# Convolution, two attentions and a mixture of experts: the expert stage begins with the image that is still on chip

## The chip, the cores and the metric

The kernel runs on one core of one Trainium2 chip. The metric is the device time in microseconds (us). The time before is 2335.57 us, the median of three runs (2335.0 to 2337.08). The engines of the core are named as the profile names them: PE multiplies matrices, and PEld is its loading of weights; DVE is the vector engine, ACT the scalar engine with its function tables, POOL is GpSimd, and SP only issues transfers.

## What is computed

Eight images of 32 x 32 pixels and 256 channels, all in 32-bit floats, pass two layers. The reference, cut to what matters here:

```python
# layer 0: group norm, 3x3 convolution (192 channels) beside 8-head attention (64 channels), residual
x = x + _L0_conv_ref(_gn(x), ...)
# layer 1: one-head attention on 1024 tokens of 256, then a mixture of experts
t = _to_tokens(x)
t = t + _L1_attn_ref(_ln_t(t), ...)
t = t + _L1_ffn_ref(_ln_t(t), ...)

def _L1_ffn_ref(x, Wr, br, W1, b1, W2, b2, gamma, beta):
    logits = jnp.mean(x, axis=1) @ Wr + br          # one row per image
    routing_weights = softmax(logits)
    expected_loads = routing_weights.sum(axis=0) * (N / B)
    scale = jnp.where(expected_loads > capacity, capacity / expected_loads, 1.0)
    routing_weights = softmax(routing_weights * scale)
    top_w, top_i = jax.lax.top_k(rw_tok, 2)         # the same two experts for all tokens of an image
    top_w = softmax(top_w)
    h = gelu(x @ W1[e] + b1[e])                     # 256 -> 512
    y = h @ W2[e] + b2[e]                           # 512 -> 256
    out = sum over the two experts of top_w * y
    return _layer_norm(out + x, gamma, beta)
```

The router takes the mean over the tokens of each normalised image, and the load of an expert is a sum over all eight images: no expert is known until the last image has left the attention.

## The kernel before

**Stages.** A loop over the images b = 0 to 7 does the convolution layer with its attention (`conv_layer_attention`) and the one-head attention (`attention_layer`), with the work of the next image filled in. An image is a tile `T[b]` of 128 x 8 x 256: eight tiles t of 128 tokens. At the end of `attention_layer` the last output tiles come from `gather` (L932) and `project` (L944, L948 to L950), which also leaves the mean and variance of every token in `mv2`. Then `root_of_tiles` (L96 to L102, two of its steps on ACT) makes one over the deviation of all eight tiles, and `mr` is mean times that. The sum over tokens of image times deviation is collected in `acc`: on POOL for images 0 to 6 (L983, L985), on DVE for image 7 (L987, L989). The image is stored to DRAM in `Td[b]` by POOL's queue (L990). `token_mean` (L995 to L1003) finishes the sum over partitions with two products on PE against ones, and `mr` with one more, and writes a column of `meanT`.

**Router.** On 8 x 8 numbers, mostly DVE: logits (L1132), a softmax (L1140 to L1144), the loads (L1151 to L1159), a second softmax, and twice the search for the largest: maximum, candidates, smallest index, one-hot row `oh`, picked weight. The indices go through PE (L1196) into the integers `idx_i`; `wbc` holds the experts' weights spread over the partitions, `dbc` the dense weights of the bias, `b1c` the chosen first biases.

**Expert stage.** For b = 0 to 7: the image comes back from `Td[b]` (L1228, loaded one image ahead on SP), SP reads the two experts of an image from `idx_i` and loads 512 KB each of first and second weights (L1237, L1241), one image ahead, in two buffers. `n2` is the normalised image (L1265, eight DVE operations), `n2T` its transpose: 16 transposes on PE into the PSUM pool `ps_t` with two buffers (L1272), copied out by DVE (L1276) and ACT (L1278). `pbr` (L1281) is the experts' second bias; POOL adds it to `n2` and beta to the image (L1286, L1287) and scales the next second weights by `wbc` (L1251). For each half q of the tokens, PE makes the hidden layer `phd` for two experts and four column groups (L1296; ACT applies Gelu, L1303), then four output tiles `py` (L1313, PSUM pool `ps_y` with three buffers); DVE adds `n2` (L1320), takes statistics (L1321), and when all four tiles of the half are there `layer_stats` makes one over the deviation (L86 to L90, the root on ACT), two operations a tile finish it (L1325, L1326), and one 512 KB transfer writes it out (L1329).

**Order.** In the loop over images PE and POOL run in the order in which the program is written (L1045); in the expert stage only POOL does (L1253), and the order of the other engines comes from a scheduler at compile time. On SP, ACT and DVE it is the scheduler's in both stages. [...]

Of the kernel before, what the change touches and what calls it, by code (L numbers as in the profile page):

```python
# [10 lines left out]
FP = mybir.dt.float32  # L11
# [25 lines left out]
def kernel(  # L37
# [38 lines left out]
    Td = [dram.tile([P, NT, C], FP, tag=f"Td{b}", name=f"Td{b}") for b in range(B)]  # L76
# [27 lines left out]
    with ExitStack() as ph:  # L104
# [24 lines left out]
        def load_image(b):  # L129
            t = work.tile([P, NT, C], FP, tag="T", name="T", bufs=2)  # L130
            eng = nc.gpsimd if b else nc.sync
            eng.dma_start(
                out=t.rearrange("p (r j) c -> p r j c", j=4), in_=xt[b].rearrange("(r p j) c -> p r j c", p=P, j=4)
            )
            return t
# [678 lines left out]
        def root_of_tiles(var):  # L814
            one_over_root(var, var, lambda n: work.tile([P, NT, 1], FP, tag=f"{n}t", name=n))

        def attention_layer(b, fill, conv, maxima):
# [133 lines left out]

            for i in range(NT):
# [17 lines left out]
            conv.run(2)  # L970
            project(NT // NIB - 1, os)


            m = mv2[:, b]
            root_of_tiles(m[:, :, 1:2])
            mr = work.tile([P, NT], FP, tag="mr", name="mr")
            nc.vector.tensor_tensor(mr, m[:, :, 0], m[:, :, 1], ALU.mult)
            acc = work.tile([P, C], FP, tag="n", name="acc", bufs=2)
            if b + 1 < B:
                part = work.tile([P, C], FP, tag="n", name="part", bufs=2)  # L980
                for t in range(NT):
                    to = part if t else acc
                    nc.gpsimd.tensor_scalar(to, T[b][:, t, :], m[:, t, 1:2], None, ALU.mult)  # L983
                    if t:
                        nc.gpsimd.tensor_tensor(acc, acc, part, ALU.add)  # L985
            else:
                nc.vector.tensor_scalar(acc, T[b][:, 0, :], m[:, 0, 1:2], None, ALU.mult)  # L987
                for t in range(1, NT):
                    nc.vector.scalar_tensor_tensor(acc, T[b][:, t, :], m[:, t, 1:2], acc, ALU.mult, ALU.add)  # L989
            nc.gpsimd.dma_start(out=Td[b], in_=T[b])  # L990
            return acc, mr

        def token_mean(b, acc, mr):

            pmt = st_tile("pmt")  # L995
            for kc in range(KC):
                nc.tensor.matmul(
                    pmt[:, kc : kc + 1], lhsT=acc[:, kc * P : (kc + 1) * P], rhs=ones[:, 0:1], start=True, stop=True
                )
# [3 lines left out]
            nc.vector.tensor_scalar(meanT[:, :, b], pmt[:, 0:KC], mrs, 1.0 / S, ALU.subtract, ALU.mult)  # L1003
# [41 lines left out]
        with tc.manual_schedule(engines={mybir.EngineType.PE, mybir.EngineType.Pool}):  # L1045
            conv = Conv(0)
            means = []
            for b in range(B):
# [49 lines left out]
                del T[b]  # L1098
# [25 lines left out]
    nc.vector.tensor_copy(iota, iota_i)  # L1124
# [21 lines left out]

    rw = sm([B, E], "rw")
# [20 lines left out]
    for k in range(TOPK):  # L1168
# [3 lines left out]
        nc.vector.tensor_scalar(cand, z, m, -float(E), ALU.is_equal, ALU.mult)  # L1172
        nc.vector.tensor_tensor(cand, cand, iota, ALU.add)
        nc.vector.tensor_reduce(idx[:, k : k + 1], cand, AX.X, ALU.min)
        nc.vector.tensor_scalar(idx[:, k : k + 1], idx[:, k : k + 1], float(E), float(E - 1), ALU.add, ALU.min)
        oh = sm([B, E], f"oh{k}")
        nc.vector.tensor_scalar(oh, iota, idx[:, k : k + 1], None, ALU.is_equal)
        hot.append(oh)
        pick = sm([B, E], f"pick{k}")
        nc.vector.tensor_tensor(pick, oh, rw2, ALU.mult)  # L1180
        nc.vector.tensor_reduce(top[:, k : k + 1], pick, AX.X, ALU.add)
        if k + 1 < TOPK:
            off = sm([B, E], f"off{k}")
            nc.vector.tensor_scalar(off, oh, 4.0, None, ALU.mult)
            z2 = sm([B, E], f"z{k}")
            nc.vector.tensor_tensor(z2, z, off, ALU.subtract)
            z = z2
    wt = sm([B, TOPK], "wt")
    softmax(wt, top, "sm3")


    prow = ps_t.tile([P, 512], FP, tag="t", name="prow")
    pw = ps_t.tile([P, 512], FP, tag="t", name="pw")
    diag = sm([B, TOPK, B], "diag")
    for k in range(TOPK):
# [3 lines left out]
        nc.vector.tensor_scalar(diag[:, k, :], ident[0:B, 0:B], wt[:, k : k + 1], None, ALU.mult)  # L1199
    nc.tensor.matmul(  # L1200
        pw[:, 0 : TOPK * B], lhsT=ones[0:B], rhs=diag.rearrange("p k b -> p (k b)"), start=True, stop=True
    )
    idx_i = small.tile([1, TOPK * B], I32, tag="idx_i", name="idx_i")
    nc.vector.tensor_copy(idx_i, prow[0:1, 0 : TOPK * B])
    wbc = sm([P, TOPK * B], "wbc")
    nc.vector.tensor_copy(wbc, pw[:, 0 : TOPK * B])
    dense = sm([B, E], "dense")
    nc.vector.tensor_scalar(dense, hot[0], wt[:, 0:1], None, ALU.mult)
    nc.vector.scalar_tensor_tensor(dense, hot[1], wt[:, 1:2], dense, ALU.mult, ALU.add)
    ptr = ps_t.tile([P, 512], FP, tag="t", name="ptr")  # L1210
    for i, m in enumerate((hot[0], hot[1], dense)):
        nc.tensor.transpose(ptr[0:E, i * B : (i + 1) * B], m, ident[0:B, 0:B])
    hotT = sm([E, (TOPK + 1) * B], "hotT")
    nc.vector.tensor_copy(hotT, ptr[0:E, 0 : (TOPK + 1) * B])
    dbc = sm([E, B, P], "dbc")
    nc.vector.tensor_copy(dbc, hotT[:, TOPK * B :].unsqueeze(2).to_broadcast([E, B, P]))

    pb = ps_t.tile([P, NF, TOPK * B], FP, tag="t", name="pb")
    for f in range(NF):
        nc.tensor.matmul(  # L1220
            pb[:, f, :], lhsT=b1sb[:, f * P : (f + 1) * P], rhs=hotT[:, 0 : TOPK * B], start=True, stop=True
        )
    b1c = sm([P, NF, TOPK * B], "b1c")
    nc.vector.tensor_copy(b1c, pb)

    def load_image(b):
        t = work.tile([P, NT, C], FP, tag="T2", name="T2")
        nc.sync.dma_start(out=t, in_=Td[b])  # L1228
        return t

    def load_experts(b):
        ws = []
        for k in range(TOPK):
            n = k * B + b
            e = nc.sync.value_load(idx_i[0:1, n : n + 1], min_val=0, max_val=E - 1)
            w1t = fw.tile([P, KC, F], FP, tag=f"w1_{k}", name=f"w1_{k}")
            nc.sync.dma_start(  # L1237
                out=w1t, in_=w1[bass.ds(e, 1), :, :].rearrange("o (k p) f -> p (o k) f", p=P)
            )
            w2t = fw.tile([P, NF, C], FP, tag=f"w2_{k}", name=f"w2_{k}")  # L1240
# [3 lines left out]
            ws.append((w1t, w2t))  # L1244
# [8 lines left out]
    ctx.enter_context(tc.manual_schedule(engines={mybir.EngineType.Pool}))  # L1253
    nxt = load_experts(0)
    scale_experts(0, nxt)
    tn = load_image(0)
    for b in range(B):
        ws, Tb = nxt, tn
        if b + 1 < B:
            tn = load_image(b + 1)  # L1260
            nxt = load_experts(b + 1)
        n2 = work.tile([P, NT, C], FP, tag="n2", name="n2")
        n2T = work.tile([P, KC, S], FP, tag="n2T", name="n2T")
        for t in range(NT):
            nc.vector.tensor_scalar(  # L1265
                n2[:, t, :], Tb[:, t, :], mv2[:, b, t, 0:1], mv2[:, b, t, 1:2], ALU.subtract, ALU.mult
            )
        for kc in range(KC):
            for q in range(2):
                tp = ps_t.tile([P, 4, P], FP, tag="t", name="tp2")  # L1270
                for j in range(4):
                    nc.tensor.transpose(tp[:, j, :], n2[:, q * 4 + j, kc * P : (kc + 1) * P], ident)  # L1272
                dst = n2T[:, kc, q * 512 : (q + 1) * 512]
                src = tp.rearrange("p j t -> p (j t)")
                if q == 0:
                    nc.vector.tensor_copy(dst, src)  # L1276
                else:
                    nc.scalar.copy(dst, src)  # L1278
# [104 lines left out]
```

## Time and profile before

The profile is one execution that took 2339.52 us, of which 2337.5 us lie between the first and the last instruction (the span). All times below are us from the start of the span.

| stretch | time | PE busy | DVE busy | ACT busy | POOL busy | PE clock | transfers, GB/s |
|---|---|---|---|---|---|---|---|
| 1750 to 1842: end of the last image's attention | 92.0 | 80.37 | 32.69 | 40.28 | 10.56 | 0.91 | 1 |
| 1842 to 1870.2: token mean, router, first transposes | 28.2 | 9.98 | 19.84 | 2.27 | 4.68 | 0.56 | 227 |
| 1870.2 to 1929.1: experts, image 0 | 58.9 | 58.90 | 14.76 | 16.86 | 16.73 | 0.98 | 53 |
| 1929.1 to 2274.8: images 1 to 6 | 345.7 | 345.70 | 159.25 | 106.47 | 93.91 | 1.00 | 70 |
| 2274.8 to 2337.5: image 7 and the end | 62.7 | 55.31 | 25.18 | 17.96 | 9.77 | 0.97 | 26 |

A row gives how long each engine was busy in the stretch. "PE clock" is the share of full speed that was granted to PE. Busy time of PE counts matmuls whose ends are modelled, so a full row doesn't mean that PE works at its peak; it does mean that no gap is seen between its instructions. A line of a timeline gives start, duration, engine and line, the operation, the tile that it writes and those that it reads, their shapes, and in brackets the idle time before it and what ended that.

### The profile page before, as it was taken

The numbers are of one execution on the slowest core, as the hardware profiler recorded it, in microseconds if no ns is written. First come the engines' busy times: TensorE is split into PE (matmuls) and PEld (weight loads), VectorE is DVE, ScalarE is ACT, GpSimd is POOL, SyncE is SP. The second block draws the span as 40 slices with busy tenths as digits, with TensorE's granted clock in tenths as the row PEclk, the third lists the DMA queues.
The fourth block names the chain that finished last, engine by engine and source line by source line (L and its number), as shares of the span: only waits on it lengthen the run. The fifth ranks groups of instructions, "written<-read, shape, count | busy, mean of one in ns | idle before, by whom it ended". The sixth has DMA issues, their size and how long they took to land. (4 is left out here: it accounts for less than half of the span.)

```text
span 2337.5 us, 41910 instructions
## 1 busy us (share of the span) xinstructions
PE 2259.4 (97%) x17273; PEld 1284.4 (55%) x17273; DVE 1481.7 (63%) x2717; ACT 955.1 (41%) x1645; POOL 505.3 (22%) x478
## 2 busy tenths in 40 slices
PE   5999999999999999999999999999998699999998
PEld 5535753664367437733763475357533566666665
DVE  7777587658756775777477748765872624444443
ACT  2255336434643563256325532553364223333332
POOL 3301240213031203300340034012301022222220
PEclk7999999999999999999999999999998799999999
DMA  3520352125122502250333025202420312222200
GB/s 105 103 50 10 58 104 39 41 48 102 22 56 42 109 5 60 56 93 3 60 89 61 7 56 105 45 27 47 82 38 1 108 50 78 78 74 78 72 37 27
DMA packets 71471, 135.85 MB, mean 58 GB/s; under 512 B 12001, under 2 KB 24169, under 8 KB 69233
## 3 DMA queue, kind: packets, MB, share of 16 engines
q1 hardware_dynamic: 65488, 115.47, 23.5%
q0 software_dynamic: 3056, 15.73, 2.0%
q8 instruction: 137, 2.24, 0.4%
q10 hardware_dynamic: 2736, 1.97, 0.3%
q14 instruction: 54, 0.43, 0.1%
HBM read 53.43 MB, written 25.17 MB: 34 GB/s over the span
## 5 line engine op out<-in xcount | busy, mean ns | idle before, releaser
L626 DVE TENSOR_REDUCE my<-lg 128x32 f32<-128x1024 f32 x512 | 617.4, 1222 | 166.3 <-PE st L658 124.9
L666 ACT ACTIVATE PT<-st 128x512 f32<-128x512 f32 (+1 forms) x944 | 542.2, 632 | 313.6 <-PE st L658 309.9
L658 PE MATMUL st<-F,km 32*128 32x512 f32 x2048 | 536.9, 640 | 8.2 <-DMA F<-mb 8.2
L618 PE MATMUL lg<-km,F 24*128 24x512 f32 x2048 | 504.9, 637 | 1.7 <-DMA F<-rh 1.7
L675 PE MATMUL po<-PT,vall 128*32 128x256 f32 (+1 forms) x3200 | 312.5, 452 | 2.4 <-ACT PT L666 2.4
L675 PEld LDWEIGHTS po<-PT,vall 128*32 128x32 f32 x3200 | 66.0, 108 | 312.8 <-issue 279.5
L618 PEld LDWEIGHTS lg<-km,F 24*128 24x128 f32 x2048 | 144.1, 183 | 163.7 <-issue 122.7
L560 PE MATMUL pc<-convw,gdif 128*128 128x192 f32 x1152 | 229.4, 342 | 0.7 <-ACT convw L309 0.7
L1296 PE MATMUL phd<-n2T,w 128*128 128x512 f32 x512 | 223.7, 595 | 0.0
L1313 PE MATMUL py<-w,hT 128*128 128x256 f32 x1024 | 223.6, 379 | 0.0
L658 PEld LDWEIGHTS st<-F,km 32*128 32x128 f32 x2048 | 175.6, 183 | 78.2 <-issue 40.5
L560 PEld LDWEIGHTS pc<-convw,gdif 128*128 128x128 f32 x1152 | 186.9, 192 | 56.4 <-issue 32.0
L1313 PEld LDWEIGHTS py<-w,hT 128*128 128x128 f32 x1024 | 194.6, 190 | 33.3 <-issue 7.7
L340 POOL TENSOR_TENSOR T<-T,l0b 128x2048 f32<-128x2048 f32 x8 | 36.3, 4534 | 617.6 <-PE tpx L333 617.6
L1320 DVE TENSOR_TENSOR r<-py,n 128x256 f32<-128x256 f32 x64 | 27.2, 425 | 213.0 <-PE py L1313 213.0
L1296 PEld LDWEIGHTS phd<-n2T,w 128*128 128x128 f32 x512 | 97.2, 191 | 116.1 <-issue 108.9
L846 POOL TENSOR_TENSOR T<-T,n 128x256 f32<-128x256 f32 x64 | 47.4, 749 | 392.4 <-DVE n L832 392.4
L1303 ACT ACTIVATE hT<-phd,b1c 128x512 f32<-128x512 f32 x128 | 86.3, 686 | 98.3 <-PE phd L1296 98.1
L569 ACT COPY m<-pc 128x384 f32<-128x384 f32 x48 | 23.0, 480 | 242.6 <-PE pc L560 198.1
L901 PE MATMUL lg<-qkv 128*128 128x512 f32 x256 | 121.1, 595 | 0.0
L910 DVE TENSOR_REDUCE nm<-lg 128x1 f32<-128x1024 f32 x64 | 78.1, 1221 | 67.5 <-PE lg L901 67.5
L932 PE MATMUL po<-pt,qkv 128*128 128x256 f32 x512 | 116.5, 380 | 0.0
(250 smaller groups left out, 2584.7 us busy)
## 6 DMA issues: line engine op xcount, KB each, us to landing
F<-rh SPq DMA_DIRECT2D x256, 128.0 KB
F<-kq SPq DMA_DIRECT2D x256, 64.0 KB
F<-rwd SPq DMA_DIRECT2D x256, 64.0 KB
w<-in_L_ffn_W_dram SPq DMA_DIRECT2D x32, 512.0 KB
rwd<-rw SPq DMA_DIRECT2D x16, 512.0 KB
Td<-T POOLq DMA_DIRECT2D x8, 1024.0 KB, 4.2
T<-Td SPq DMA_DIRECT2D x8, 1024.0 KB
out_dram<-yo SPq DMA_DIRECT2D x16, 512.0 KB
```

What stands on the lines that cost most here:

```text
L560: nc.tensor.matmul(pc[:, v, :], lhsT=gflat[:, 2 * pair + v, kc, at : at + P], rhs=convw[:, 2 * pair + v, dy, kc * CO : (kc + 1) * CO], sta ...
L618: nc.tensor.matmul(lg[:, a, :], lhsT=self.F[r : r + 24, a, 0, i * P : (i + 1) * P], rhs=KM[self.g][r : r + 24, a].rearrange("p e k -> p (e ...
L626: nc.vector.tensor_reduce(my[:, :, hl], lg.rearrange("p a (y x) -> p y a x", y=WW), AX.XY, ALU.max)
L658: nc.tensor.matmul(st[:, i, :] if len(heads) > 1 else st, lhsT=KM[self.g][r : r + 32, a, e, :], rhs=self.F[r : r + 32, a, e, :], start=Tru ...
L666: nc.scalar.activation(self.pts[j][:, hs, :], st, AF.Exp)
L675: nc.tensor.matmul(self.po[32 * hl : 32 * hl + 32, cols], lhsT=vall[:, j, h * (DH + 1) : h * (DH + 1) + 32], rhs=self.pts[j][:, hl, cols], ...
L901: nc.tensor.matmul(lg[:, h, :], lhsT=qk[0][:, i * P : (i + 1) * P], rhs=qk[1][:, h * 512 : (h + 1) * 512], start=True, stop=True,)
L910: nc.vector.tensor_reduce(nm, lg, AX.X, ALU.max, negate=True)
L932: nc.tensor.matmul(po[:, 0:IB], lhsT=v1[:, jc, :], rhs=pt[:, jc, :], start=jc == 0, stop=jc == NT - 1)
L1296: nc.tensor.matmul(phd, lhsT=ws[k][0][:, kc, f * P : (f + 1) * P], rhs=n2T[:, kc, q * 512 : (q + 1) * 512], start=kc == 0, stop=kc == KC - 1,)
L1303: nc.scalar.activation(hT[:, k * NF + f, :], phd, AF.Gelu, bias=b1c[:, f, k * B + b : k * B + b + 1])
L1313: nc.tensor.matmul(py, lhsT=hT[:, k * NF + f, j * P : (j + 1) * P], rhs=ws[k][1][:, f, :], start=k == 0 and f == 0, stop=k == TOPK - 1 and ...
```

## The change

The seven parts below all lie between the end of the last image's attention and the end of the kernel, apart from `token_mean`, which all images use.

1. The images' tiles get a pool of their own (`tokens`, two buffers), which the expert stage uses too. The last image is neither stored nor loaded again; the expert stage takes the images in the order 7, 0, 1, ..., 6. Image 0 is loaded before the stage begins, into the buffer that image 6 has left.
2. The last image's sum over tokens is made by PE: for each tile and each half of the channels one product of the tile with the column of one over the deviation, summed in PSUM. The first six tiles come before the last `project`, the last two after it. The deviations are made in the same two parts.
3. In `token_mean` two DVE operations write `meanT`, one for each half of the channels, where there was one.
4. From the router on, DVE, PE and POOL run in the order in which the program is written.
5. In the router the candidates are one operation instead of two (`iota` holds the index minus 8), so are the numbers for the second search, and the picked weights, the third softmax and everything that hangs on them stand behind the indices. `weigh_experts` (diag, `pw`, `wbc`, dense weights, `dbc`) stands between the first and the second expert of the first image; so do the transposes of that image's second half.
6. In the expert stage the first weights of both experts are loaded ahead of the second weights. The bias product, the additions on POOL and the scaling stand behind the first expert of the first half (`beside`). The next image is normalised after the first half's hidden layer and transposed between the second and the third output tile of the second half.
7. At the very end the last half is finished in two steps: three output tiles, then the fourth, each with its own transfer.

```diff
@@ attention_layer, end
+            def sum_tiles(part):
+                if not sums_of:
+                    sums_of.extend(lg_tile(f"pm{kc}")[:, 0, :] for kc in range(KC))
+                for t in range(part.start, part.stop):
+                    for kc in range(KC):
+                        nc.tensor.matmul(
+                            sums_of[kc][:, 0:1],
+                            lhsT=T[b][:, t, kc * P : (kc + 1) * P],
+                            rhs=mv2[:, b, t, 1:2],
+                            start=t == 0,
+                            stop=t == NT - 1,
+                        )
...
             conv.run(2)
+            if b + 1 == B:
+                deviation(slice(0, NT - NIB))
+                sum_tiles(slice(0, NT - NIB))
             project(NT // NIB - 1, os)
...
+                nc.gpsimd.dma_start(out=Td[b], in_=T[b])
             else:
-                nc.vector.tensor_scalar(acc, T[b][:, 0, :], m[:, 0, 1:2], None, ALU.mult)
-                for t in range(1, NT):
-                    nc.vector.scalar_tensor_tensor(acc, T[b][:, t, :], m[:, t, 1:2], acc, ALU.mult, ALU.add)
-            nc.gpsimd.dma_start(out=Td[b], in_=T[b])
+                deviation(last_two)
+                sum_tiles(last_two)
+                acc = sums_of
@@ router
+    ctx.enter_context(
+        tc.manual_schedule(engines={mybir.EngineType.DVE, mybir.EngineType.PE, mybir.EngineType.Pool})
+    )
...
-        nc.vector.tensor_scalar(cand, z, m, -float(E), ALU.is_equal, ALU.mult)
-        nc.vector.tensor_tensor(cand, cand, iota, ALU.add)
+        nc.vector.scalar_tensor_tensor(cand, z, m, iota, ALU.is_equal, ALU.mult)
...
+    first = two_tiles()
+    normalised(B - 1, last, range(4), first[0])
+    transposed(*first, 0)
...
+    def weigh_experts():
+        normalised(B - 1, last, range(4, NT), first[0])
+        transposed(*first, 1)
+        pw = ps_y.tile([P, 512], FP, tag="y", name="pw")
+        diag = sm([B, TOPK, B], "diag")
+        for k in range(TOPK):
+            nc.vector.tensor_scalar(diag[:, k, :], ident[0:B, 0:B], wt[:, k : k + 1], None, ALU.mult)
+        nc.tensor.matmul(
+            pw[:, 0 : TOPK * B], lhsT=ones[0:B], rhs=diag.rearrange("p k b -> p (k b)"), start=True, stop=True
+        )
+        nc.vector.tensor_copy(wbc, pw[:, 0 : TOPK * B])
...
@@ expert stage
+    images = [B - 1, *range(B - 1)]
...
+                if q == 0 and k == 0:
+                    if not at:
+                        weigh_experts()
+                    beside()
+            if q == 0 and after is not None:
+                coming = two_tiles()
+                normalised(after, tn, range(NT), coming[0])
...
+            ends = (3, 4) if after is None and q else (4,)
             for j in range(4):
+                if j == 2 and q and after is not None:
+                    for half in range(2):
+                        transposed(*coming, half)
...
+                if j + 1 not in ends:
+                    continue
+                lo = 0 if j + 1 == ends[0] else ends[0]
+                layer_stats(st[:, lo : j + 1], mv[:, lo : j + 1], j + 1 - lo, 1e-5)
...
+                nc.sync.dma_start(out=to[:, lo : j + 1], in_=y[:, lo : j + 1])
```

The new helper `transposed`, for one half q of the tokens:

```python
    def transposed(n2, n2T, q):
        for kc in range(KC):
            tp = ps_t.tile([P, 4, P], FP, tag="t", name="tp2")
            for j in range(4):
                nc.tensor.transpose(tp[:, j, :], n2[:, q * 4 + j, kc * P : (kc + 1) * P], ident)
            dst = n2T[:, kc, q * 512 : (q + 1) * 512]
            src = tp.rearrange("p j t -> p (j t)")
            if kc == 0:
                nc.vector.tensor_copy(dst, src)
            else:
                nc.scalar.copy(dst, src)
```

## The prediction

> **What bounds the kernel now.** I read the engine totals and the 40 slices of the page first: TensorE (PE) is the bound nearly everywhere, and only slices 30 and 31 (58 us each) show it idle and its clock throttled.
>
> ```profile
> PE 2259.4 (97%) x17273; PEld 1284.4 (55%) x17273; DVE 1481.7 (63%) x2717; ACT 955.1 (41%) x1645; POOL 505.3 (22%) x478
> ...
> PE   5999999999999999999999999999998699999998
> ...
> PEclk7999999999999999999999999999998799999999
> ```
>
> Then the timeline of PE there and in the expert stage (start, duration, line, idle time before it and who ended it):
>
> ```profile
> 1841.17 1.13 PE L944 MATMUL pa<-wo,os 128*128 128x256 f32 x4 [0.52 <-ACT os L936]
> 1849.79 1.01 PE L997 MATMUL pmt<-ones,acc 128*128 128x1 f32 x4 [7.48 <-DVE acc L989]
> ...
> 1870.24 15.20 PE L1296 MATMUL phd<-n2T,w 128*128 128x512 f32 x32
> 1885.27 13.98 PE L1313 MATMUL py<-w,hT 128*128 128x256 f32 x64
> ...
> 1926.63 1.04 PE L1272 MATMUL tp<-ident,n 128*128 128x128 f32 x8
> 1927.60 0.69 PE L1281 MATMUL pbr<-b2sb,dbc 8*128 8x256 f32 x2
> 1928.22 1.09 PE L1272 MATMUL tp<-ident,n 128*128 128x128 f32 x8
> 1929.15 13.90 PE L1296 MATMUL phd<-n2T,w 128*128 128x512 f32 x32
> ```
>
> Two things are to be seen. Between the last attention matmuls (1841.2) and the first expert matmul (1870.24) lie 29 us in which PE mostly waits for DVE. From there it never waits: image after image has a period of 57.62 us (1929.15 to 1986.77), of which 2.52 us (1926.63 to 1929.15) are the 16 transposes and the bias matmul `pbr` between two images. What is saved ahead of 1870 is saved at the end; whatever is added to PE's stream after it is added, seven times if it is in the image loop.
>
> **Part by part.** Only the last image's attention tail, the router and the expert stage change.
>
> *Token mean by PE.* Now DVE sums eight tiles (L987 and L989, 1845.74 to 1849.74) and meanT is ready at 1851.70. Changed: PE sums twelve products of the first six tiles before L944, four of the last two after it. A product is two passes; with the clock full, four such passes of L997 cost 0.50 us (the next line's weights start at 322.80, theirs at 322.30), so 0.125 each. Twenty-four passes are 3.0 us, from 1840.5: L944 starts at 1843.5, 2.3 later. Their root fits in DVE's idle time after 1839.0 (row L96 to L102: 1.47 us). Behind L944 DVE's chain keeps its length up to the root (1845.63 now, 1847.93 then), then eight passes (1.0), the last product to meanT (1850.60 to 1851.70: 1.10) and one more 0.22 us meanT operation: 1850.3. **Saves 1.4 us**; 0.6 if the clock has fallen by then (0.22 a pass, as in the L997 row above). The other seven images get one more 0.22 us meanT operation, beside PE-bound work: nothing.
>
> *Router.* From the second softmax's differences (1855.18) to the indices `idx_i` (1859.04) are 3.86 us. Fused candidates, the sums of picked weights moved behind, and no n tiles between save about 1.3; but the fixed order puts the reciprocal and the scaling, which wait for ACT until 1855.54, ahead of the maximum: +0.8. **Saves 0.5.** `idx_i` then ends at 1857.1.
>
> *First expert matmul.* The first weights go out 1.21 us after `idx_i` (1859.04, 1860.25), so at 1858.35. For their landing the nearest rows are the windows of the DMA: 0.5 MB needs till about 2.9 us after its issue, and a wait ends 1.3 us after the data (flow ends at 1944.6, DVE goes on at 1945.96): 1862.5. Transposed input: pb (1.89 us, 1863.61 row) after hotT from 1857.8, eight cold transposes (1.97), the second copy on ACT (0.59): 1862.3. **Matmuls from 1862.5 instead of 1870.24.**
>
> *What follows it.* Here the gain is mostly given back. (a) Clock: the first three passes now come 0.86 us apart instead of 0.43 until 1872.9, a loss of 1.3, after five us of small PE work just ahead. The Trainium skill, "TensorE: Matmul & The Clock Gate", section "The HAM clock gate", says that full speed comes only after a busy window of about 3.4 us of a free-running clock; with little work ahead that is 3.4 to 6.8 us at half speed, a loss of 1.7 to 3.4. By the row 1.3, by the rule some 2.2; I take 2.2, since the change removes the work that the row's window held. (b) Between the first and second expert, `weigh_experts` puts a serial chain into PE's queue: 8 transposes (1.04), with DVE's copy ending at +1.35, diag (0.35), pw, its copy and two dense operations (to +2.85), a transpose, hotT and dbc (0.67; to +4.0), pbr (0.43): 4.5 us in which PE does 1.7. Lower bound 2.5 (if the copies didn't queue), upper 6 (clock falls again). First L1313: 1862.5 + 6.87 + 2.2 + 4.5 + 6.87 = 1882.9, against 1885.27: **−2.3**. POOL scales the second weights (2 × 2.85) from 1874.0 to 1879.7, before they are used; that they are loaded behind both first weights costs nothing for the same reason. The store of the last image, no longer made, held up only the load that is gone too.
>
> *Transposes inside the loop.* They move from between two images to between the second and third output tile of the second half, both halves in a row, with two PSUM buffers. The third group needs the buffer that DVE's copy frees, and in the fixed order that copy stands behind this tile's sum and statistics:
>
> ```profile
> 2295.70 0.42 DVE L1320 TENSOR_TENSOR r<-py,n 128x256 f32<-128x256 f32 x1 [1.76 <-PE py L1313]
> 2296.16 0.43 DVE L1321 BATCH_NORM_STATS2 fst<-r 128x6 f32<-128x256 f32 x1
> ...
> 2273.92 0.85 PEld L1272 LDWEIGHTS tp<-ident,n 128*128 128x128 f32 x8 [0.33 <-DVE n2T L1276]
> ```
>
> PE's slots of that tile end at 2295.49 (2288.59 + 32 × 0.2157). The copy would run from 2296.62 to 2297.31, +1.82; PE goes on 0.26 later (now: copy ends 2273.66, weights 2273.92), and eight transposes take 0.95: 3.03. With pbr elsewhere (0.45): 3.5 instead of 2.52, now filled by pbr and by transposes of the other half. **+0.97 an image, seven times: +6.8**; 5.4 if PE goes on at once.
>
> *Moved loads.* Image 0 is loaded into image 6's buffer, behind the third fold's F<-mb (1720.95) and ahead of the last fold's in SP's queue; the DMA is busy 2% there (1720 to 1752), and the buffer's last use is long past: nothing. If it were not, that fold would stand behind it and PE wait at L658. Later images' loads go out when the previous image's last tiles are done, +7 us in an image, and land by +13 (6.3 us, 1939.63 to 1945.96); L1265 needs them before the first sum at +17.4. The skill ("SBUF — State Buffer", "Who interferes with whom") says that a DVE tensor_scalar in a two-port mode, and DVE operations with two SBUF inputs, stand still for a whole GpSimd operation. The second shows here: L1326 takes up to 2.58 us against 0.48. The first does not: 0.41 us each, and two took 0.73 while POOL scaled (1867.19). By the rule L1265's eight would end near +24, by the row at +16; py has three buffers, its fourth tile starts at +24.1, so either costs PE nothing.
>
> *Last sums.* After the third tile DVE normalises three (six operations near 0.45), so the fourth's sum starts 5.1 us after the third tile instead of 3.66, and the last output is ready 4.6 us after PE ends instead of 3.76 (2329.94, 2333.70): +0.8. The last transfer has 128 KB instead of 512 (1.35 us of data): −1.0. **−0.2.**
>
> *Sum:* −2.3 + 6.8 − 0.2 = +4.3, on a span of 2337.5 (profiled time 2339.5). The median of the runs is 2335.57, 4 below; the same difference gives **2339.9** (+0.18%).
>
> **Rivals.**
> 1. *The transposes don't stall* (the copy gets ahead of the statistics, or a release is quicker): 7 × (2.4 − 2.52) = −0.8, total −3.3: 2332.3. For it: PE has slack for nothing else. Against it: DVE's order is fixed by hand. Faster beyond the bound only if the chain in `weigh_experts` also costs under 3.2 us instead of 4.5.
> 2. *Slower, by the clock*: PE is so little busy in that chain that the clock falls; the second expert's first passes are then at half speed, +2.2, and with weights 1 us late +7.5: 2343. It decides from the point where no window of 3.4 us has enough work; the trace shows the clock falling 3.4 us after the last matmul (1842.3, half by 1845.8), so with gaps under 1 us I hold it the weaker.
> 3. *The early load does harm*: PE waits at L658 in the last fold for 1 MB ahead of it, +5: 2345. Against: 25 us of quiet between the folds.
>
> **Numbers.** Forecast 0.58, rival 1 0.2, rival 2 0.14, rival 3 and the unseen 0.08. A measurement of this kernel tells from no change about 0.2% (4.7 us). The forecast lies just under it, its own range +2 to +7 splits half and half; rival 1 is mostly within, a part faster; 2 and 3 are slower. Slower 0.48, same 0.39, faster 0.13. Range 2332.5 to 2345.5.
>
> **What would show it.** First L1296-like matmul near 1862.5; a PE gap near 4.5 us between the two experts of the first image; in every other image 3 us for the block of transposes with an idle wait on DVE's n2T copy; L944 near 1843.5; the last output about 4.6 us after PE. Wrong if the block takes 2 us, if the first py starts before 1880, or if the stretch before 1839 moves.

## The result, and the profile after

The changed kernel takes 2346.48 us (median of five, 2342.33 to 2347.55) against 2335.57 (median of five too, 2335.00 to 2337.08): a ratio of 1.0043, 95% interval 1.0028 to 1.0058. Measured again (e5 below, 12 runs against 27) the ratio is 1.0029, interval 1.0019 to 1.0039, or 6.8 us. It is slower, as the likeliest sign said, by more than the 4.3 us forecast, and the first median lies outside the range; the second, 2344.48, lies inside.

The page of the profiled execution (2346.51 us, span 2344.7) against the lines shown of before:

```profile
PE 2267.7 (97%) x17301; PEld 1288.0 (55%) x17301; DVE 1473.8 (63%) x2723; ACT 956.0 (41%) x1648; POOL 501.8 (21%) x477
...
PE   5999999999999999999999999999998799999998
...
PEclk7999999999999999999999999999998899999999
```

PE is busy 8.3 us longer with only 28 more instructions: the page sees a slower PE, not more work. Where it is slower, only the timeline tells. PE there, from the last attention work to the second expert of the image that now comes first:

```profile
1848.06 1.87 PE L974 MATMUL pm<-mv,T 128*128 128x1 f32 x8 [3.37 <-DVE mv L107]
...
1862.72 8.55 PE L1377 MATMUL phd<-n2T,w 128*128 128x512 f32 x16 [1.47 <-DVE sm_s L1216]
1871.11 1.04 PE L1187 MATMUL tp<-ident,n 128*128 128x128 f32 x8
1872.75 0.39 PE L1304 MATMUL pw<-diag,ones 8*128 8x16 f32 x2 [0.60 <-DVE diag L1303]
1874.64 0.17 PE L1312 MATMUL ptr<-ident,dense 8*8 8x8 f32 x1 [1.50 <-DVE dense L1310]
1875.77 1.14 PE L1361 MATMUL pbr<-b2sb,dbc 8*128 8x256 f32 x2 [0.96 <-DVE dbc L1314]
```

The first expert starts at 1862.72 instead of 1870.24. Then come three waits for DVE, and the second expert begins only at 1876.83. The granted clock in this stretch (columns: window, its length, busy time and instructions of PE, PEld, DVE, ACT, POOL, then PE's clock, DMA share, GB/s):

```profile
1872.00:1874.00 2.00, 0.54 (x4) 0.29 (x2) 1.48 (x6) 0.59 (x1) 0.54 (x1) 1.00 0.33 107
1874.00:1876.00 2.00, 0.40 (x2) 0.31 (x3) 1.70 (x4) 0.00 (x0) 2.00 (x1) 0.97 0.00 0
1876.00:1878.00 2.00, 2.00 (x4) 0.84 (x4) 2.00 (x3) 0.37 (x1) 2.00 (x2) 0.50 0.00 0
1878.00:1880.00 2.00, 2.00 (x4) 0.86 (x3) 2.00 (x5) 0.00 (x0) 2.00 (x1) 0.50 0.00 0
1880.00:1882.00 2.00, 2.00 (x3) 0.67 (x2) 2.00 (x2) 0.69 (x1) 2.00 (x2) 0.50 0.00 0
```

PE is busy 0.94 us of the first four, and from 1876 the clock is half. The second expert's 16 passes take 9.88 us (1876.83 to 1886.71) instead of 6.97, which the same work takes in e1 below.

To compare profiles whose earlier parts differ, I count from the start of the last attention `po` (L938; L932 before), the last work of PE that no kernel here touches. Times in us; "first py" is the first output tile's first pass.

| profile | that po starts | to 1st expert | 1st expert | between | 2nd expert | to first py | first to last py | last py to end |
|---|---|---|---|---|---|---|---|---|
| before | 1837.04 | 33.20 | 15.03 with 2nd | - | - | 48.23 | 430.86 | 21.37 |
| before, again (e10) | 1832.63 | 33.22 | 14.97 with 2nd | - | - | 48.19 | 430.87 | 21.31 |
| after | 1837.30 | 25.42 | 8.39 | 5.72 | 9.88 | 49.41 | 437.46 | 20.53 |
| after, again (e5) | 1836.76 | 24.94 | 8.92 | 5.29 | 8.66 | 47.81 | 437.46 | 20.57 |

("Last py" is the start of the last 64-pass block.) In the profiled pair the stage is +1.18 up to the first py, +6.60 over the images and -0.84 at the end: +6.94, and with 0.26 ahead of it the 7.2 us between the spans. In the second profile of after it is -0.42, +6.60, -0.80: +5.4. Two profiles of before agree to 0.09 us; those of after differ by 1.6 us, and that is the length of the second fall: 1.22 us in the second expert and 0.43 in `pbr` ahead of it. (The first expert starts 0.48 later in the first profile and takes 0.53 less, because the clock comes back 2.9 us behind its start there, at 1865.6, and 4.0 behind it in e5, at 1865.7.)

The other part of the 10.9 us lies in code that the change doesn't touch. PE's clock also falls elsewhere, in one execution and not in another. Windows of after, then of the first profile of before, then of its second:

```profile
316.00:320.00 4.00, 4.00 (x28) 3.02 (x27) 3.73 (x5) 0.36 (x1) 3.67 (x6) 1.00 0.09 17
320.00:324.00 4.00, 4.00 (x20) 2.14 (x21) 2.85 (x7) 1.80 (x4) 3.31 (x4) 0.85 0.54 131
324.00:328.00 4.00, 4.00 (x17) 2.56 (x12) 1.82 (x3) 1.78 (x4) 0.00 (x0) 0.50 0.95 242
...
328.00:332.00 4.00, 4.00 (x14) 0.72 (x16) 1.78 (x3) 1.09 (x2) 0.00 (x0) 0.50 1.04 161
```

```profile
60.00:64.00 4.00, 2.28 (x7) 0.85 (x6) 0.48 (x1) 1.20 (x2) 3.08 (x4) 0.97 0.60 129
64.00:68.00 4.00, 4.00 (x9) 2.50 (x9) 1.97 (x2) 0.00 (x0) 0.00 (x0) 0.50 0.55 85
```

```profile
60.00:64.00 4.00, 3.50 (x12) 1.48 (x11) 0.73 (x1) 1.54 (x2) 2.66 (x4) 1.00 0.61 132
64.00:68.00 4.00, 4.00 (x23) 2.46 (x22) 1.82 (x3) 0.00 (x0) 0.41 (x1) 1.00 0.55 82
```

The fall in after makes the stretch of L623 to L680 behind it last 33.7 us (320.02 to 353.70) where before takes 29.1. Before's first profile (2339.52 us) lost some 3.2 us against its second (2334.98) around 64, and 1 us more at another fall, from 1753.4 to 1756.8; the last po is 4.4 us apart and everything behind it the same.

So the change itself is worth 5.4 to 6.9 us by the profiles, 6.8 by the ratio of e5. The other 4 us or so of the first comparison are of the size of such falls: the first five times of before lie at 2335 to 2337, while 27 later ones have a median of 2339.41 (2334.34 to 2340.99); of after, four lie at 2346 to 2348 and one at 2342.33. Which of those ten times had which fall is not recorded, except for the one that was profiled, so this part is argued and not shown.

### The profile page after: what moved, and what is told of

It reads as the page before. It is cut to its first block, busy times and chain, and to the rows that moved or that the text cites. A ratio compares the mean times of both kernels' runs of the same rounds, so it can differ in the third digit from the quotient of the medians.

```text
span 2344.7 us, 41981 instructions
## 1 busy us (share of the span) xinstructions
PE 2267.7 (97%) x17301; PEld 1288.0 (55%) x17301; DVE 1473.8 (63%) x2723; ACT 956.0 (41%) x1648; POOL 501.8 (21%) x477
## 5 line engine op out<-in xcount | busy, mean ns | idle before, releaser
L623 PE MATMUL lg<-km,F 24*128 24x512 f32 x2048 | 506.4, 639 | 0.3 <-DMA F<-rh 0.3
L680 PE MATMUL po<-PT,vall 128*32 128x256 f32 (+1 forms) x3200 | 312.6, 452 | 2.9 <-ACT PT L671 2.4
L680 PEld LDWEIGHTS po<-PT,vall 128*32 128x32 f32 x3200 | 66.1, 108 | 314.3 <-issue 280.5
L623 PEld LDWEIGHTS lg<-km,F 24*128 24x128 f32 x2048 | 144.9, 183 | 162.5 <-issue 125.3
L1377 PE MATMUL phd<-n2T,w 128*128 128x512 f32 x512 | 228.9, 603 | 1.5 <-DVE sm_s L1216 1.5
L938 PE MATMUL po<-pt,qkv 128*128 128x256 f32 x512 | 116.5, 380 | 0.0
```

The source lines that it names most:

```text
L623: nc.tensor.matmul(lg[:, a, :], lhsT=self.F[r : r + 24, a, 0, i * P : (i + 1) * P], rhs=KM[self.g][r : r + 24, a].rearrange("p e k -> p (e ...
L680: nc.tensor.matmul(self.po[32 * hl : 32 * hl + 32, cols], lhsT=vall[:, j, h * (DH + 1) : h * (DH + 1) + 32], rhs=self.pts[j][:, hl, cols], ...
L938: nc.tensor.matmul(po[:, 0:IB], lhsT=v1[:, jc, :], rhs=pt[:, jc, :], start=jc == 0, stop=jc == NT - 1)
L1377: nc.tensor.matmul(phd, lhsT=ws[k][0][:, kc, f * P : (f + 1) * P], rhs=n2T[:, kc, q * 512 : (q + 1) * 512], start=kc == 0, stop=kc == KC - 1,)
```

## The experiments

All start from after's code (e10 from before's). The same columns for the changed kernels:

| profile | ratio to before, interval | to 1st expert | 1st expert | between | 2nd expert | to first py | first to last py | last py to end |
|---|---|---|---|---|---|---|---|---|
| e1 busy PE | 1.0022 (1.0016 to 1.0029) | 25.18 | 8.85 | 5.32 | 6.97 | 46.32 | 437.46 | 20.58 |
| e2 chain spread | 1.0001 (0.9992 to 1.0009) | 25.01 | 10.99 with between | - | 6.97 | 42.97 | 437.47 | 20.61 |
| e3 transposes split | 1.0000 (0.9991 to 1.0008) | 25.05 | 8.80 | 5.33 | 8.58 | 47.76 | 431.22 | 20.58 |
| e4 one end | 1.0033 (1.0020 to 1.0045) | 25.01 | 8.90 | 5.28 | 8.66 | 47.85 | 437.47 | 23.29 |
| e5 after again | 1.0029 (1.0019 to 1.0039) | 24.94 | 8.92 | 5.29 | 8.66 | 47.81 | 437.46 | 20.57 |
| e6 e2 and e3 | 0.9965 (0.9952 to 0.9978) | 25.05 | 10.83 with between | - | 6.97 | 42.85 | 431.21 | 20.59 |
| e7 sum by DVE | 1.0031 (1.0021 to 1.0041) | 26.12 | 9.93 | 5.28 | 8.67 | 50.00 | 437.45 | 20.54 |
| e8 dense first | 1.0013 (1.0005 to 1.0022) | 25.00 | 8.70 | 3.78 | 8.67 | 46.15 | 437.46 | 20.56 |
| e9 e6, busy PE | 0.9977 (0.9969 to 0.9984) | 26.50 | 9.00 with between | - | 6.97 | 42.47 | 431.21 | 20.59 |
| e11 e6, busy otherwise | 0.9963 (0.9949 to 0.9977) | 24.02 | 9.51 with between | - | 6.97 | 40.50 | 431.21 | 20.56 |
| e12 e6 again | 0.9985 (0.9978 to 0.9992) | 25.15 | 10.69 with between | - | 6.97 | 42.81 | 431.21 | 20.58 |

Ratios carry the falls elsewhere too; the trace columns are the finer instrument, and the verdicts below rest on them. Each row is one execution: e6 and e12, the same kernel, differ by 0.14 us at most in these columns, and after's two profiles as said above.

**e1: the chain as it is, PE kept busy in its waits.**

```diff
         transposed(*first, 1)
+        busy(1)          # then busy(3) behind pw, busy(2) behind the transpose of dense
...
+def busy(n):
+    spare = ps_h.tile([P, 512], FP, tag="h", name="spare")
+    for _ in range(n):
+        nc.tensor.matmul(spare[:, 0:256], lhsT=ws[0][0][:, 0, 0:P], rhs=n2T[:, 0, 0:256], start=True, stop=True)
```

> The kernel after, with six idle-filling matmuls (128x256, two passes of 0.216 us each, their sums unused) put into PE's three waits inside weigh_experts: one after the transposes, three after pw, two after the transpose of dense. The chain of DVE operations is not touched. Clock theory (PE too little busy there, so that the clock falls at 1875.9 and the second expert's first seven passes come 0.86 apart): the clock stays full, the second expert takes 6.9 us instead of 9.9, the first py starts near 1883.3 instead of 1886.7, the span is 3.4 shorter. Rival (only the length of the chain counts, the clock's fall has another reason, for instance a period of its own): second expert again 9.9, first py at 1886.7 or up to 0.5 later, span unchanged.

The same windows as above:

```profile
1872.00:1874.00 2.00, 1.83 (x13) 1.37 (x12) 1.21 (x5) 1.15 (x2) 0.00 (x0) 1.00 0.36 114
1874.00:1876.00 2.00, 2.00 (x10) 1.44 (x9) 1.67 (x4) 0.00 (x0) 1.98 (x1) 1.00 0.00 0
1876.00:1878.00 2.00, 2.00 (x7) 0.86 (x7) 2.00 (x4) 0.37 (x1) 2.00 (x2) 1.00 0.00 0
```

PE is busy 3.83 us of the first four instead of 0.94, and the clock stays full. The chain is as long as in e5 (5.32 and 5.29), but the second expert takes 6.97 us. So the second loss is the clock's, and that PE has so little work there is what brings it down. In the second expert it costs 2.9 us in the first profile of after and 1.7 in e5. Windows of half a microsecond tell why; first the two in which the clock turns in after, then the two of e5:

```profile
1875.50:1876.00 0.50, 0.23 (x1) 0.23 (x2) 0.50 (x2) 0.00 (x0) 0.50 (x1) 0.88 0.00 0
...
1882.50:1883.00 0.50, 0.50 (x2) 0.16 (x1) 0.50 (x1) 0.00 (x0) 0.50 (x2) 0.79 0.00 0
```

```profile
1875.50:1876.00 0.50, 0.50 (x3) 0.17 (x2) 0.50 (x1) 0.00 (x0) 0.50 (x1) 0.94 0.00 0
...
1879.00:1879.50 0.50, 0.50 (x2) 0.08 (x1) 0.50 (x1) 0.00 (x0) 0.50 (x1) 0.65 0.00 0
```

The clock is at half from 1875.88 to 1882.71 in the one, 6.83 us, and from 1875.94 to 1879.35 in the other, 3.41 us (worked out from the share of the window in which it turns). The half clock comes in pieces of 3.4 us, here one or two, and a piece full of matmuls costs 1.7. The traces' own record of the clock bears this out: in all fourteen, every stretch at half clock that ends inside the span is a whole multiple of 3.41 us, from 3.41 to 27.3, and so is every stretch at full clock between two of them. So the clock turns only on a beat of 3.41 us.

**e2: the chain taken out of PE's way.**

```diff
+    diag ... ; dense ...                      # DVE, directly behind wt
+    normalised(B - 1, last, range(4, NT), first[0])
+    def weigh_experts(f):
+        if f == 1: pw, wbc, transpose of dense, hotT, dbc
+        if f == 2: transposed(*first, 1)
...
-                if q == 0 and k == 0:
-                    if not at: weigh_experts()
+                    if q == 0 and k == 0 and not at:
+                        weigh_experts(f)      # inside the loop over f
```

> The kernel after, with weigh_experts taken apart: diag and dense by DVE right behind wt, pw and the transpose of dense behind the first expert's second block of matmuls, the eight transposes of the half behind its third, so that every one of them finds its input ready. PE still does the same work there. Theory (the 5.7 us between the experts are waits, and they bring the clock down): what is left is PE's own work, 1.04 + 0.4 + 0.2 + 0.6 and up to 0.1 for each return to the matmuls, about 2.6 us, all at full clock: first py near 1880.6 instead of 1886.7, span 6 shorter. Rival 1 (the clock falls all the same): 1883.6, span 3 shorter. Rival 2 (the first py now waits for POOL's scaling of the second weights, which can't begin before their landing at 1873.4): POOL ends near 1880.4, the py of the second expert's half waits for it, span 5 shorter at least, with a wait on POOL shown.

First py at 42.97 us, 4.8 below e5 and 6.4 below the first profile of after. PE's work is the same; the first expert with all of it takes 10.99 us against 14.2 for both in e5, and the clock doesn't fall:

```profile
1873.83 0.69 PE L1364 MATMUL pbr<-b2sb,dbc 8*128 8x256 f32 x2
1874.45 7.13 PE L1380 MATMUL phd<-n2T,w 128*128 128x512 f32 x16
1881.42 13.98 PE L1411 MATMUL py<-w,hT 128*128 128x256 f32 x64
```

No `py` waits, so POOL's scaling held up nothing.

**e3: the transposes in two parts.** The block as it is in after:

```profile
1921.16 1.04 PE L1187 MATMUL tp<-ident,n 128*128 128x128 f32 x8
1921.36 0.42 DVE L1415 TENSOR_TENSOR r<-py,n 128x256 f32<-128x256 f32 x1 [2.50 <-PE py L1408]
1921.82 0.43 DVE L1416 BATCH_NORM_STATS2 fst<-r 128x6 f32<-128x256 f32 x1
1922.16 0.67 DVE L1191 COPY n2T<-tp 128x512 f32<-128x512 f32 x1
1922.23 0.58 ACT L1193 COPY n2T<-tp 128x512 f32<-128x512 f32 x1 [7.09 <-PE tp L1187]
...
1922.87 1.09 PE L1187 MATMUL tp<-ident,n 128*128 128x128 f32 x8 [0.68 <-ACT n2T L1193]
...
1923.80 1.46 PE L1408 MATMUL py<-w,hT 128*128 128x256 f32 x6
```

PE waits until both copies are done (DVE's ends at 1922.83, ACT's at 1922.81), and DVE's has indeed stood behind the sum and the statistics. The block takes 2.64 us.

```diff
-                if j == 2 and q and after is not None:
-                    for half in range(2):
-                        transposed(*coming, half)
+                if j >= 2 and q and after is not None:
+                    transposed(*coming, j - 2)
```

> The kernel after, with the next image's transposes in two parts: half 0 ahead of the third tile, half 1 ahead of the fourth, eight passes each, so that no group has to wait for a PSUM buffer that DVE's or ACT's copy has still to free. Theory (0.7 us of the block of 2.64 are a wait for those copies): two parts of 0.97 each, 0.7 less an image, period 57.9 instead of 58.56, span 4.9 shorter. Rival (each break in the py stream costs a refill of its own of 0.1 to 0.3 us and the wait only moves): 0 to 0.3 less an image, span 0 to 2 shorter.

```profile
1918.06 1.04 PE L1187 MATMUL tp<-ident,n 128*128 128x128 f32 x8
1918.93 3.62 PE L1407 MATMUL py<-w,hT 128*128 128x256 f32 x16
1922.39 1.04 PE L1187 MATMUL tp<-ident,n 128*128 128x128 f32 x8
1923.26 3.62 PE L1407 MATMUL py<-w,hT 128*128 128x256 f32 x16
```

Two parts of 0.87 us, no wait: 1.74 instead of 2.64. From first to last py it is 6.24 us less, 0.89 an image, more than expected, and the images cost what they cost before the change (431.22 against 430.86).

**e4: one step at the end.**

```diff
-            ends = (3, 4) if after is None and q else (4,)
+            ends = (4,)
```

> The kernel after, with the last half's sums finished in one step of four tiles, as before the change. By the comparison of the two traces (end of PE's last slot to the end of the span: 7.56 us before, 6.72 after) the span grows by 0.84. By the prediction's sum (last output 0.8 later against a shorter last transfer, 1.0) it grows by 0.2.

Both missed: the end grows by 2.72 us against e5, not by 0.84 or 0.2. The last of eight operations of DVE, and then the last transfer, in e4; then the same of after:

```profile
2336.64 0.49 DVE L1425 SCALAR_TENSOR_TENSOR yo<-r,fmv,T 128x256 f32<-128x256 f32 x1
2337.16 0.33 SPq L1428 DMA_DIRECT2D out_dram<-yo  x1
```

```profile
2339.18 0.42 DVE L1415 TENSOR_TENSOR r<-py,n 128x256 f32<-128x256 f32 x1
2339.29 2.87 SPq L1428 DMA_DIRECT2D out_dram<-yo  x2
...
2341.32 0.48 DVE L1425 SCALAR_TENSOR_TENSOR yo<-r,fmv,T 128x256 f32<-128x256 f32 x1
```

In e4 PE's last slot ends at 2331.42 (2317.61 + 13.81), and all eight operations stand behind it, in the written order, until 2337.13. In the kernel before, a scheduler ordered DVE, and three of the first four (r times gamma) stood ahead of the last tile's sum, at 2321.00, 2324.38 and 2327.84. So the fixed order alone would have cost 1.9 us at the end (23.29 against 21.37); the two steps pay that back and 0.8 more.

**e5: after once more.**

> The kernel after once more, unchanged. In its first profile the granted clock fell to 0.5 from 322.9 to 333 us, in the second image, which cost about 4.5 us there; no other profile so far, before's among them, shows it, and none of that code is touched. Theory (chance: such falls come where PE is briefly little busy and do not belong to the change): the runs lie on two levels about 4 us apart, near 2342 and 2346, the lower one with no fall at 322, and the ratio to before comes out nearer to 1.003 than to 1.0043. Rival (the change moves the program so that the fall at 322 comes nearly always): nearly all runs near 2346 and a ratio of 1.0043 again.

The theory holds in part: the fall at 322 is gone, another one, from 63.5 to 70.3, has come, and the ratio is 1.0029; but the times spread over 2340.2 to 2351.3 without two clear levels. The fall at 322 is back in the profile of e11 (clock 0.50 from 324 to 332) and in no other here. Two of twelve profiles of changed kernels have it, neither of the two of before; whether the change makes it likelier is open.

**e6 and e12: both repairs.**

> The kernel after, with both edits: the parts of weigh_experts spread over the first expert's matmuls, and the transposes in two halves ahead of the third and the fourth tile. If the two gains are independent (about 6.4 us up to the first py, 0.89 us in each of seven images) the expert stage from the first py on takes what it took before, the first py comes 43.0 us after the last attention matmuls' start (48.2 before the change, 49.4 after it), and the kernel is faster than before by about 5.2 + 0.8 - 0.4 = 5.6 us, a ratio near 0.998. Rival (the gain ahead of the first py only moves a wait to POOL's scaling of the weights): first py block longer than 13.9 with a wait on POOL, ratio 0.999 to 1.000.

> The kernel of the two edits once more, beside e11 on one chip, because its first ratio (0.9965) comes from five runs. By its trace against before's (5.4 us earlier at the first py, 0.35 us later by the last, 0.8 less at the end: 5.8 us) the ratio should be 0.9975; 0.9965 was then helped by the level of its runs.

The gains are independent: first py at 42.85 and 42.81 us, 431.21 over the images. By the trace the kernel is 5.8 us faster than before, 0.9975; the ratios are 0.9965 and 0.9985, one on each side. That it is faster than before, both intervals say.

**e7: the weighted sum by DVE, as before.**

> The kernel after, with the last image's weighted token sum by DVE over eight tiles, as before the change; nothing else. By the two traces (from the start of the last attention po to meanT's end: 14.66 us before, 13.64 after) meanT comes 1.0 later and everything behind it 1.0 later, if the clock falls and rises in the same places. By the prediction (1.4 saved) 1.4 later. If PE's sums change when the clock falls or comes back, the first expert's matmuls show another loss than 1.5 us.

The first expert comes 1.18 us later than in e5 (0.70 than in the first profile of after), and loses another 1.0 to the clock. So the sum by PE saves about 1.1. The ratios (1.0031 and 1.0029) don't tell the two apart.

**e8: DVE's dense operations ahead of POOL's start.**

```diff
-        nc.vector.tensor_copy(wbc, pw[:, 0 : TOPK * B])
         dense = sm([B, E], "dense")
...
         nc.vector.tensor_copy(dbc, ...)
+        nc.vector.tensor_copy(wbc, pw[:, 0 : TOPK * B])
```

> The kernel after, with the copy of pw to wbc, which lets POOL begin to scale the second weights, moved behind DVE's dense, hotT and dbc. The same operations. Theory (DVE's scalar_tensor_tensor with two operands in SBUF stood still while POOL began, 1.07 us instead of 0.20): it takes 0.2 again, pbr starts 1.5 earlier because wbc is also out of the chain, the part between the two experts takes 4.0 instead of 5.7. If the clock still falls, the first py comes 1.7 earlier; if 4.0 us are too short for it, 4.7 earlier. Rival (the 1.07 has another cause, for instance waiting for its own operand): it stays at 1.0 and the part takes 5 us.

The operation in after, beside POOL, and then in e8:

```profile
1873.46 6.94 POOL L1341 TENSOR_SCALAR w<-w,wbc 128x1024 f32<-128x1024 f32 x2 [28.51 <-DMA w<-in_L_ffn_W_dram]
1873.52 1.07 DVE L1310 SCALAR_TENSOR_TENSOR dense<-oh,wt,dense 8x8 f32<-8x8 f32 x1
```

```profile
1868.39 0.21 DVE L1309 SCALAR_TENSOR_TENSOR dense<-oh,wt,dense 8x8 f32<-8x8 f32 x1
```

0.21 us instead of 1.07, and the chain 3.78 instead of 5.29 (of the 1.51, 0.65 is the copy to `wbc`, which no longer stands ahead of the dense operations): the two-operand DVE operation was held while POOL worked. It was held for 0.86 us, not for the 3.5 that one of POOL's two operations took. The clock falls all the same, from 1871.72 to 1875.13 (3.41 us, 8.67 for the second expert), although PE's timeline shows work in 2.3 us of the 3.78, and in 2.45 of the 3.41 us ahead of the fall. Shortening the chain was not enough, and how much work PE needs to keep its clock the runs do not tell.

**e9 and e11: both repairs, PE kept busy through the router.** e9 put filling matmuls behind the last `pa`, behind `logits`, `pload` and the first transposes; e11 changed their places.

```diff
                 deviation(last_two)
+                spare = st_tile("spare")
+                for _ in range(7):
+                    nc.tensor.matmul(spare[:, 0:C], lhsT=ident, rhs=wo, start=True, stop=True)
                 sum_tiles(last_two)
...
+    busy(3)             # e11: behind plog; busy(5) behind pload, busy(1) behind the first prow
     transposed(*first, 0)
+    busy(3)             # 5 in e9
```

> The kernel of the two edits together, with idle-filling matmuls (128x256, sums unused) in PE's waits from the last attention tile to the first expert: seven behind the last pa, three behind plog, five behind pload, five behind the first transposes. The chain of DVE and ACT is not touched. Theory (the clock is down there only because PE does little, and costs its cold passes: about 0.9 us in the last eight pm passes, 1.0 in pb and the first transposes, 1.5 to 2 in the first expert's matmuls): the clock stays full from 1836 on, the indices come about 1.2 us earlier, the first expert's matmuls wait for their weights and then come 0.43 apart from the start, and the first py comes 39.5 to 40.5 us after the last po instead of 42.85; the ratio to before is about 0.0012 lower than with the two edits alone. Rival (the fillers delay the small matmuls behind them and cost what they save, or the weights set the first expert anyway and the clock is the smaller part): first py 42 to 43.

> The kernel of e9 with the idle-filling matmuls in other places: three behind plog (e9's went ahead of it and held it up by 1.5 us), five behind pload, one behind the first prow, only three behind the first transposes (e9's five held up the first expert by 0.9). Theory: nothing on the path is held up now and the clock stays full, so the first expert's matmuls start some 23.8 us after the last po's start instead of 25.05, need 7.0 us without cold passes, and the first py comes near 40.3 instead of 42.85. Rival (weights' landing is the bound and has not moved, only the cold passes go): first py near 41.0 to 41.2. If PE is still too little busy for its clock, 42.5 again.

e9 missed: the group behind `logits` ran ahead of `plog` and its last past the arrival of the weights, so that the first expert came 1.4 us later; only the cold passes were gone (9.00 against 10.83). With the fillers behind the critical matmuls e11's first py comes at 40.50, 2.3 below e12, as the theory said. In this stretch its clock falls only between 1856 and 1864 (0.82 and 0.76). By these columns it is the fastest kernel here; its ratio, 0.9963, is clear of e12's, measured beside it, but not of e6's.

**e10: before once more.**

> The kernel before once more, for a second profile. Its first profile was 2339.5 us, four above the median of its runs, with the clock at 0.5 near 60 to 70 us, which three of the profiles of changed kernels (those whose last po starts near 1832) don't show. Theory (the two levels of its runs differ by whether the clock falls there): a run near 2335 shows a full clock there, one near 2339.5 shows it fallen; everything behind the last po is the same to 0.5 us except the first expert's cold passes.

As expected behind the last po (first table) and near 64; the fall at 1753, worth 1 us of the 4.4, was not in the expectation.

## Why the prediction missed

- **Token mean, saves 1.4**: meanT ends 13.64 us after the last po's start, 14.66 before: 1.0, because the last passes were cold (0.22 each), between its two cases of 1.4 and 0.6. *Router, 0.5*: together they should put the end of `idx_i` at 1857.1; it came at 1857.28, with the last po 0.26 later. *First expert at 1862.5*: 1862.72. This half of the sum held.
- **Clock, a loss of 2.2 in the first expert**: 1.4 and 2.0 (8.39 and 8.92 against 6.97). Rule and row bracket it; right.
- **"4.5 us in which PE does 1.7"**: 5.72 and 5.29. The term missing in it is DVE's dense operation, 0.86 longer beside POOL (e8); the 0.43 that 5.72 has more is `pbr` at half clock. The prediction had the rule for it from the Trainium skill ("SBUF — State Buffer", "Who interferes with whom": an operation with two SBUF inputs contends with a GpSimd instruction that reads SBUF) and weighed it only for `n2`, where it hides; it did not carry it to the one such operation in the serial chain.
- **The step of the sum that failed is the one set aside as rival 2, "the weaker"**: no term for a second fall of the clock stood in the sum. It fell in every profile that holds the chain on idle PE (after, e3, e4, e5, e7, e8) and cost 1.6 to 2.9 us in the second expert, 0.43 more in after's `pbr`; with PE kept busy (e1) or the chain spread (e2, e6, e9, e11, e12) it cost nothing. The argument was that gaps under 1 us are shorter than the 3.4 us the trace shows from the last matmul to the fall. The longest gap came to 1.50 us, still shorter; it was the little work in all of them, 0.94 us in the four before 1876, that went with the fall. The skill's section that the prediction had cited for the return ("TensorE: Matmul & The Clock Gate", "The HAM clock gate") has the clock set by free-running windows of some 3.4 us; the pieces of 3.41 and 6.83 us agree. It names an idle window for the fall; e8 shows that the window need not be idle.
- **The step that took the time out of the range is the last, "the same difference gives 2339.9"**: it treated the 4 us between before's profiled time and its median as a fixed offset. e10 shows what they were: falls of the clock around 64 and at 1753 in that one execution, 4.4 us together. A later median of before is 2339.41; after's profiled execution took as long as its median (2346.51, 2346.48) and had a fall of its own, at 322. With +5.4 to +6.9 the rest of the sum is still inside the range.
- **First py, -2.3**: +1.18 in the profiled pair, -0.42 in e5, by the longer chain and the second fall.
- **Transposes, +6.8**: +6.60, for the reason given (DVE's copy behind sum and statistics). Its parts were off against each other: the block 2.64 instead of 3.03, because the copy started 1.00 us after PE's slots ended instead of 1.13 and PE went on 0.04 after it, not 0.26. `pbr` costs 0.81 instead of 0.45: 0.62, and 0.19 because 32 passes of `phd` cut in two take 6.96 and 6.97 instead of 13.74.
- **Last sums, -0.2**: -0.84. The last transfer came out as said (2.9 us from the last output to the end, 3.8 before), but the last output is 3.82 us after PE, hardly later than the 3.76 of before.
- **Moved loads and DVE's `n2` beside POOL, nothing**: right for the time. But "the first does not show" was wrong for the new order: the same operation takes 0.41 us at the median in the trace of before, and 1.17, up to 2.57, in after's, where it runs beside POOL's additions (2.43 beside one of 2.40 at 1943.5).

Terms of the sum, then: -2.3 became +1.2 or -0.4, +6.8 became +6.6, -0.2 became -0.8. That gives +5.4 to +6.9 instead of +4.3. The direction was right, and by far the largest term of it, the transposes, for the reason given.

## To carry to other kernels

Before moving small dependent steps into the queue of a busy PE, add up how much work is left to it in each few microseconds: if it is as little as here (0.94 us in four; even 2.45 in 3.41), the matmuls behind them can run at half clock too, and the price is the chain plus that. Issue such steps between matmuls, each late enough that its input is ready, and split a block of transposes to as many groups as there are PSUM buffers. When the order of an engine is fixed by hand, look at what its scheduler had done at the end of the program, where nothing hides a late operation.

## What had not been expected of the hardware

- One kernel's executions lie several us apart (before: 2334.36 to 2340.66 in 43 runs; after: 2340.18 to 2351.32 in twelve). Two profiles of before differ by 4.4 us ahead of the last po, the slower one at half clock from 63.8 to 70.6 and from 1753.4 to 1756.8; after's fall at 322 made a stretch of 29.1 us (before) last 33.7. Some of these falls lie where PE is short of work (1.51 us in the 3.41 ahead of 1753.4), but not all: ahead of the fall at 322.8 the windows show PE busy throughout, 4.00 of 4.00. What the clock counts as work stays open.
- Six idle-filling matmuls, worth nothing to the result, save about 1.5 us (e1 against e5); nineteen save 2.3 (e11 against e12); e9's, of which some stood ahead of a matmul that was waited for, saved 0.3.
